# Four weight sums made by VectorE between the closing's steps instead of by GpSimd, and seven block products in another order

## The chip, the cores and the metric

One Trainium2 chip; the kernel runs on one of its cores, in one launch. The metric is the device time of that launch in microseconds, the median of several runs; lower is better.

## What is computed

Two graph layers on x (3327 rows of 1024 features) with a dense adjacency matrix. The first quantises a normalised x and a weight to few levels, multiplies them, and multiplies the adjacency matrix by the result. The second is attention with 8 heads of 64 features under the mask adj > 0, and then an MLP of four dense layers; its result is added to x1, the first layer's output. What matters for the change is the end of the second:

```python
att = softmax(where(adj > 0, leaky_relu(e_src + e_dst), NEG))
h   = elu(einsum('hnm,hmd->hnd', att, Wh))
enc = transpose(h, (1, 0, 2)).reshape(n, 512)
out = relu(enc @ W1.T + b1)        # 512 -> 256
out = relu(out @ W2.T + b2)        # 256 -> 256
out = relu(out @ W3.T + b3)        # 256 -> 512
return x1 + (out @ W4.T + b4)      # 512 -> 1024
```

## The kernel before

The 3327 rows are padded to 26 tiles of 128. Up to about 126 us the kernel makes the quantised support, up to about 900 us it multiplies by the adjacency matrix (line 730) and makes the heads' features, and from about 910 us it attends (line 1134). The MLP fills the rest, from 1918 us on. The four engines with queues of their own matter here: TensorE (PE), VectorE (DVE), ScalarE (ACT) and GpSimd (POOL); most DMAs are issued on the queue of SyncE (SP).

*Who sets the order.* The program is traced in Python, and a planner then orders each engine's instructions by readiness under costs of its own. An instruction that is not tied may be put ahead of earlier traced ones. `pin` (`tc.keep_in_program_order`) ties an instruction behind the one traced just before it on its engine; `issue_after` and `queue_behind` tie single pairs. [...]

*Attention.* `attends` (line 787) lists 32 steps: two halves of the target rows, four pairs of heads, the two heads of a pair, two sub-blocks of 6 or 7 row tiles. Each step runs over 26 source tiles: VectorE makes a selection `sel` from `srow`, `ndst` and the mask (line 1109), TensorE multiplies it into 6 or 7 accumulators (line 1134). At the end ScalarE copies these to `xs` (line 1152).

*Closing.* `close(i)` (line 924) is a generator that finishes a step, one piece for each call of `close_more` (line 976): VectorE adds the halves of `xs` to `su` (936) and ScalarE scales its upper half by `ratio` (939); VectorE forms `dn` (941); adds `up` (943); takes a reciprocal (946), with which ScalarE scales and goes through the elu (949, 951, 952); VectorE ends the elu (956), ScalarE splits the words (`eh`, 962), and GpSimd's queue writes them to `enc_d` in DRAM (964). All the VectorE pieces are pinned. Closings run during the next step; that of the last step has none behind it, and the loop at line 1155 runs it through, five calls.

*First group ahead.* During the last step the MLP's weights and biases are loaded and layer 1 of the first group of four row tiles is multiplied (`first_layer`, line 1058).

*MLP.* It goes by groups of four row tiles (the last has two). `dense` (line 1166) makes layers 1 to 3 with features on partitions; ScalarE evicts each 128 features from PSUM with bias and relu (line 1186). For the first group layers 2 and 3 are called ahead of the loop (lines 1280 and 1281), with `by_input=True`, which pins their matmuls. `joined` (line 1191) loads a later group's features from `enc_d` with two transposing DMAs (line 1039) and joins the half words with four ScalarE copies (line 1197). `load_x1` (line 1043) loads the rows of x1 into `nodes`; there are two buffers.

*Layer 4.* It takes two row tiles at a time in `rows_out` (line 1235). The two tiles and the two halves of the 512 inputs and of the 1024 outputs make a 2 x 2 by 2 x 2 block product, which is done with seven products of 128x512 outputs in place of eight ("1" to "7"). For that, four sums over the weight W4 are needed once: `t1` to `t4`, 128x1024 each (lines 1208 to 1211; `t1` overwrites a part of the weight, `t2` to `t4` lie where the last mask was, shown as "mask" in the profile), made by GpSimd; and four sums over the activations for each group, `combined` (line 1216), in the space of `enct0` (shown as "rest"). Each product is two passes over k in one of four PSUM banks (`o_ps`); the results are folded into the x1 rows `x11` to `x22`, to which the bias `bb4` is added first (line 1239), and `leave` (line 1245) makes an output half row and issues its DMA, on SP and, for an odd end of rows, on ScalarE's queue. Products "1", "6" and "5" are first copied to SBUF by ScalarE (line 1258), which frees their banks. `gaps` puts the next group's layers between the products.

Of the kernel before, what the change touches and what calls it, by code (L numbers as in the profile page):

```python
# [8 lines left out]
F32 = mybir.dt.float32  # L9
# [6 lines left out]
ALU = mybir.AluOpType  # L16
# [4 lines left out]
P = 128  # L21
# [4 lines left out]
F = 1024  # L26
KF = F // P
FC = F // 512
# [33 lines left out]
def two_layer_kernel(  # L62
# [23 lines left out]
    nc = tc.nc  # L86
# [81 lines left out]
    with tc.tile_pool(name="at", bufs=2, reuse_waits="tile") as atp:  # L168
# [42 lines left out]
        with tc.tile_pool(name="s1", bufs=2, reuse_waits="tile") as s1, tc.tile_pool(  # L211
# [9 lines left out]
            def pin(ins):  # L221
                tc.keep_in_program_order(ins)
# [574 lines left out]
    with tc.tile_pool(name="srow0", bufs=1, reuse_waits="tile") as srow0, tc.tile_pool(  # L797
# [178 lines left out]
        def close_more():  # L976
            if closing and closing[0][1] <= done:
                gen = closing[0][0]
                need = next(gen, None)
                closing[0] = gen, need  # L980
                if need is None:
                    closing.pop(0)
# [18 lines left out]
        for i, (c, g, e, si) in enumerate(attends):  # L1001
# [150 lines left out]
                freed = nc.scalar.copy(xs[:, b], accs[b].rearrange("p (q c) -> p q c", q=2))  # L1152
            gen = close(i)
            closing.append((gen, next(gen)))
        while closing:
            close_more()


    with tc.tile_pool(name="s4", bufs=2, reuse_waits="tile") as s4, tc.tile_pool(
        name="s4_ps", bufs=4, space=PSUM, reuse_waits="tile"  # L1160
    ) as ps_p, tc.tile_pool(name="s4_o", bufs=4, space=PSUM, reuse_waits="tile") as o_ps:

        enc_x1.append(nodes("nodes1"))
        groups = [range(t0, min(t0 + 4, T)) for t0 in range(0, T, 4)]

        def dense(xt, wt, bt, cols, tag, by_input=False):


            k_n, m_n = wt.shape[1], wt.shape[2] // P
            yt = s4.tile([P, m_n, 512], F32, tag=tag, name=tag)  # L1170
            order = [(k, m) for m in range(m_n) for k in range(k_n)]
            pss = {}
            for k, m in sorted(order) if by_input else order:
                if k == 0:
                    pss[m] = ps_p.tile([P, 512], F32, tag="ps", name=f"{tag}_ps")
                ins = nc.tensor.matmul(  # L1176
                    pss[m][:, :cols],
                    wt[:, k, m * P : (m + 1) * P],
                    xt[:, k, :cols],
                    start=(k == 0),  # L1180
                    stop=(k == k_n - 1),
                )
                if by_input:
                    tc.keep_in_program_order(ins)
                if k == k_n - 1:
                    nc.scalar.activation(
                        yt[:, m, :cols], pss[m][:, :cols], AF.Relu, bias=bt[:, m : m + 1]
                    )
            return yt

        def joined(g):

            load_encoded(g % 2, groups[g])
            xt = s4.tile([P, EMB // P, 512], F32, name="enct")
            n = len(groups[g]) * P
            for k in range(EMB // P):
                nc.scalar.copy(halves_of_words(xt[:, k, :n]), by_feature(enc_x1[g % 2][0], n)[:, :, k])  # L1197
            return xt

        w4c = [[w4[:, 2 * k : 2 * k + 2, c * 512 : (c + 1) * 512] for c in range(FC)] for k in range(2)]  # L1200
        t2, t3, t4 = (
            masks[1].rearrange("p b j i -> p (b j i)").bitcast(F32)[:, n * F : (n + 1) * F].rearrange(
                "p (k c) -> p k c", k=2
            )
            for n in range(3)
        )
        t1 = w4c[0][1]
        nc.gpsimd.tensor_tensor(t3, w4c[1][1], w4c[0][1], ALU.subtract)
        nc.gpsimd.tensor_tensor(t1, w4c[0][1], w4c[0][0], ALU.subtract)
        nc.gpsimd.tensor_tensor(t2, w4c[1][1], t1, ALU.subtract)  # L1210
        nc.gpsimd.tensor_tensor(t4, w4c[1][0], t2, ALU.subtract)
        sums = enct0.rearrange("p k c -> p (k c)").rearrange(
            "p (s k t i) -> p s k t i", s=4, k=2, t=2
        )

        def combined(h3, n):

            at = h3[:, :, : 2 * n * P].rearrange("p k (t e i) -> p k t e i", e=2, i=P)
            (a11, a21), (a12, a22) = [[at[:, 2 * k : 2 * k + 2, :, e] for e in range(2)] for k in range(2)]
            s1, s2, s3, s4_ = (sums[:, q, :, :n] for q in range(4))  # L1220
            nc.vector.tensor_tensor(s1, a21, a22, ALU.add)
            nc.vector.tensor_tensor(s2, s1, a11, ALU.subtract)
            nc.vector.tensor_tensor(s3, a11, a21, ALU.subtract)
            nc.vector.tensor_tensor(s4_, a12, s2, ALU.subtract)
            return {
                "1": (a11, w4c[0][0]),
                "2": (a12, w4c[1][0]),
                "3": (s4_, w4c[1][1]),
                "4": (a22, t4),
                "5": (s1, t1),  # L1230
                "6": (s2, t2),
                "7": (s3, t3),
            }

        def rows_out(tiles, x1, of, q, gaps):

            x0 = x1[:, q : q + 2]
            for e in range(2):
                nc.vector.tensor_tensor(x0[:, e], x0[:, e], bb4, ALU.add)
            (x11, x12), (x21, x22) = [  # L1240
                [x0[:, e, c * 512 : (c + 1) * 512] for c in range(FC)] for e in range(2)
            ]
            yo = [s4.tile([P, F], F32, name="yo", bufs=3) for _ in tiles]

            def leave(e, c, one, other):
                t, cs = tiles[e], slice(c * 512, (c + 1) * 512)
                nc.vector.tensor_tensor(yo[e][:, cs], one, other, ALU.add)
                for queue, r in zip((nc.sync, nc.scalar), row_pieces(t)):
                    queue.dma_start(out[t * P + r.start : t * P + r.stop, cs], yo[e][r, cs])

            kept = {b: s4.tile([P, 512], F32, name="p" + b, bufs=1) for b in "165"}
            for n, b in enumerate("1426573"):
                st, mv = of[b]
                ps = o_ps.tile([P, 512], F32, tag="o", name="o")
                for k in range(2):
                    nc.tensor.matmul(ps, st[:, k, q // 2], mv[:, k], start=(k == 0), stop=(k == 1))  # L1256
                if b in kept:
                    nc.scalar.copy(kept[b], ps)
                if b == "4":
                    nc.vector.tensor_tensor(x21, x21, ps, ALU.add)  # L1260
                elif b == "2":
                    nc.vector.tensor_tensor(x11, x11, ps, ALU.add)
                    leave(0, 0, kept["1"], x11)
                elif b == "6":
                    nc.vector.tensor_tensor(kept["6"], kept["6"], kept["1"], ALU.add)
                    nc.vector.tensor_tensor(x12, x12, kept["6"], ALU.add)
                elif b == "5":
                    nc.vector.tensor_tensor(x12, x12, kept["5"], ALU.add)
                    nc.vector.tensor_tensor(x22, x22, kept["5"], ALU.add)
                elif b == "7":  # L1270
                    nc.vector.tensor_tensor(kept["6"], kept["6"], ps, ALU.add)
                    leave(1, 0, kept["6"], x21)
                    leave(1, 1, kept["6"], x22)
                elif b == "3":
                    leave(0, 1, ps, x12)
                if n in gaps:
                    gaps[n]()

        encs = {1: joined(1)}
        h = dense(h1_0, w2, bb2, len(groups[0]) * P, "h2", by_input=True)  # L1280
        h3 = dense(h, w3, bb3, len(groups[0]) * P, "h3", by_input=True)
        for g, tiles in enumerate(groups):
            following = []
            if g + 1 < len(groups):
                load_x1((g + 1) % 2, groups[g + 1])
                if g + 2 < len(groups):
                    encs[g + 2] = joined(g + 2)
                following = [(w1, bb1, "h1"), (w2, bb2, "h2"), (w3, bb3, "h3")]
                h = encs.pop(g + 1)
            of = combined(h3, len(tiles) // 2)  # L1290

            def next_layer():
                nonlocal h
                wt, bt, tag = following.pop(0)
                h = dense(h, wt, bt, len(groups[g + 1]) * P, tag)

            at = [(0, 6), (1, 2), (1, 5)] if g == 0 else [(0, 2), (0, 6), (1, 2)]
            for pair in range(len(tiles) // 2):
                gaps = {n: next_layer for p, n in at if following and p == pair}
                rows_out(tiles[2 * pair : 2 * pair + 2], enc_x1[g % 2][1], of, 2 * pair, gaps)  # L1300
            h3 = h
# [43 lines left out]
```

## Time and profile before

| | us |
|---|---|
| runs, median of 3 | 2197.64 (2196.57 to 2198.72) |
| profiled execution, its own time | 2197.31 |
| its span, first to last instruction | 2195.4 |
| TensorE busy | 2154.9 |
| VectorE busy | 1627.1 |
| ScalarE busy | 1135.0 |
| GpSimd busy | 189.1 |
| last step's last matmul ends, layer 2 of the first group begins on TensorE | 1917.84 |
| first block product begins | 1936.69 |

The table and all the lines below come from one profiled execution. A timeline line has the start in us, the busy time, the engine, the line of the kernel and the operation, the tile written and the tiles read with their shapes, the number of instructions merged, and in brackets the idle time before it with what ended that.

### The profile page before, as it was taken

What the parts mean: (1) busy time and instruction counts of PE and PEld (TensorE: products, weight loads), DVE (VectorE), ACT (ScalarE), POOL (GpSimd) and SP (SyncE); (2) the same over time, 40 slices, a digit from 0 to 9 for tenths busy, and PEclk for the clock granted to TensorE, in tenths of its full rate; (3) what the DMA queues carried; (4) which work ended last, traced back from release to release, by engine and by line L of the source; (5) the groups of instructions that cost most, each with busy time, mean ns of one, the idle gap of its engine ahead of it and who ended that gap; (6) DMA issues with size and microseconds to landing.
All of it is one profiled execution on the core that took longest, in us unless ns stands there. A gap on an engine that the chain in (4) does not pass through costs nothing.

```text
span 2195.4 us, 31473 instructions
## 1 busy us (share of the span) xinstructions
PE 2154.9 (98%) x12405; PEld 1738.8 (79%) x12405; DVE 1627.1 (74%) x2144; ACT 1135.0 (52%) x1754; POOL 189.1 (9%) x273
## 2 busy tenths in 40 slices
PE   5999999999999999999999999999999999989999
PEld 2477777777777777799999999999999999834444
DVE  8845555554555555789999999999999999965445
ACT  6734445454454444466656656565656555452321
POOL 2301010111111101100000000000000000110000
PEclk9999999999999999999999999999999999999999
DMA  6654566556655556944242341655242332463222
GB/s 220 163 184 149 171 188 185 158 170 172 186 186 162 165 174 186 297 159 150 88 142 88 109 125 30 224 178 157 88 143 87 119 116 55 126 162 125 93 99 72
DMA packets 246036, 321.16 MB, mean 146 GB/s; under 512 B 105268, under 2 KB 187396, under 8 KB 245888
## 3 DMA queue, kind: packets, MB, share of 16 engines
q1 hardware_dynamic: 225276, 245.91, 36.9%
q0 software_dynamic: 20544, 73.18, 10.6%
q8 instruction: 97, 1.59, 0.3%
q14 instruction: 51, 0.42, 0.1%
q10 hardware_dynamic: 68, 0.06, 0.0%
HBM read 208.72 MB, written 86.79 MB: 135 GB/s over the span
## 4 chain that ended last, share of the span: by engine, by line
PE 86%; DVE 6%; DMA 5%; ACT 2%; issue 1%; SPq 0%; POOL 0%; DVEq 0%; ACTq 0%; POOLq 0%
PE acc L1134 29%; PE mm L730 22%; PE mps L883 15%; PE o L1256 7%; PE whm L641 6%; PE h_ps L1176 4%; PE mm L337 3%; DMA at<-in_adj_t 2%; DMA yht<-yh 2%; DVE lo L189 1%; DMA w<-in_w 0%; ACT enct L1197 0%; DVE prod L655 0%; DVE stats L141 0%; DVE fw L697 0%
## 5 line engine op out<-in xcount | busy, mean ns | idle before, releaser
L1109 DVE SCALAR_TENSOR_TENSOR sel<-srow,ndst,mask 128x896 fp32r<-128x896 f32 (+1 forms) x832 | 864.2, 1080 | 40.6 <-PE acc L1134 34.8
L883 PE MATMUL mps<-dw,mf 128*128 128x260 f32 x2704 | 453.6, 283 | 0.0
L730 PE MATMUL mm<-s_int,hi 128*128 128x512 f32 x1352 | 426.3, 396 | 0.0
L730 PE MATMUL mm<-s_int,lo 128*128 128x512 f32 x1352 | 416.7, 389 | 0.0
L1134 PE MATMUL acc<-f_even,sel 128*128 128x260 f32 x2704 | 396.8, 284 | 0.8 <-DVE sel L1109 0.8
L1134 PE MATMUL acc<-f_odd,sel 128*128 128x260 f32 x2704 | 394.1, 286 | 0.4 <-DVE sel L1109 0.4
L876 ACT CAST mf<-mask 128x1664 fp32r<-128x1664 uint8 x208 | 331.4, 1593 | 112.6 <-PE mps L883 98.3
L883 PEld LDWEIGHTS mps<-dw,mf 128*128 128x128 f32 x2704 | 377.5, 188 | 0.2 <-ACT part L897 0.2
L1134 PEld LDWEIGHTS acc<-f_odd,sel 128*128 128x128 f32 x2704 | 352.6, 188 | 7.9 <-issue 2.9
L1134 PEld LDWEIGHTS acc<-f_even,sel 128*128 128x128 f32 x2704 | 354.8, 188 | 4.2 <-DVE sel L1109 1.3
L730 PEld LDWEIGHTS mm<-s_int,hi 128*128 128x128 f32 x1352 | 253.9, 188 | 62.6 <-issue 11.5
L730 PEld LDWEIGHTS mm<-s_int,lo 128*128 128x128 f32 x1352 | 253.6, 188 | 53.1 <-DVE lo L189 0.3
L189 DVE TENSOR_TENSOR lo<-at,hi 128x896 fp32r<-128x896 f32 x104 | 106.2, 1021 | 156.3 <-ACT hi L185 156.2
L641 PE MATMUL whm<-whead,ht 128*128 128x512 f32 x416 | 182.7, 592 | 0.0
L190 DVE TENSOR_SCALAR mk<-at 128x896 uint8<-128x896 f32 (+1 forms) x104 | 61.5, 593 | 143.3 <-DMA at<-in_adj_t 143.3
L185 ACT CAST hi<-at 128x896 fp32r<-128x896 f32 x104 | 92.2, 887 | 131.6 <-PE mm L730 96.3
L641 PEld LDWEIGHTS whm<-whead,ht 128*128 128x128 f32 x416 | 78.8, 190 | 89.1 <-issue 87.1
L897 ACT COPY part<-mps 128x260 f32<-128x260 f32 x103 | 39.0, 379 | 189.6 <-PE mps L883 189.6
L964 POOL DMA_DIRECT2D enc_d<-eh x64 | 57.6, 904 | 901.6 <-ACT eh L962 901.1
L612 ACT COPY ht<-yht 128x1024 uint16<-128x1024 uint16 x50 | 67.7, 1355 | 72.8 <-DMA yht<-yh 72.8
L337 PE MATMUL mm<-w_int,xqt 128*128 128x512 bf16 x416 | 94.4, 383 | 6.6 <-DVE w_int L468 4.5
L648 ACT ACTIVATE wht<-whm,lnr 128x512 f32<-128x512 f32 x26 | 18.0, 691 | 144.4 <-PE whm L641 138.0
(195 smaller groups left out, 1894.2 us busy)
## 6 DMA issues: line engine op xcount, KB each, us to landing
feat_d<-fw POOLq DMA_DIRECT2D x26, 1040.0 KB, 5.3
f_even<-feat_d SPq DMA_DIRECT2D x7, 3380.0 KB, 13.8
f_odd<-feat_d SPq DMA_DIRECT2D x7, 3380.0 KB, 12.7
at<-in_adj_t SPq DMA_DIRECT2D x52, 448.0 KB, 4.3
at<-in_adj_t SPq DMA_DIRECT2D x52, 384.0 KB, 4.0
dw<-dsum_d SPq DMA_DIRECT2D x16, 910.0 KB, 9.2
dsum_d<-dw POOLq DMA_DIRECT2D x26, 520.0 KB, 6.2
x_d<-xt POOLq DMA_DIRECT2D x26, 512.0 KB, 6.7
```

The lines of the kernel that those rows point to most:

```text
L185: ins = nc.scalar.copy(hi, at)
L189: nc.vector.tensor_tensor(lo, at, hi.bitcast(F32), ALU.subtract)
L337: nc.tensor.matmul(mms[t][:, r], xqts[t][:, k, :], w_int[:, k, r], start=(k == 0), stop=(k == KF - 1))
L612: nc.scalar.copy(halves_of_words(ht[:, c * KF // FC : (c + 1) * KF // FC].rearrange("p k i -> p (k i)")), yht.rearrange("p (two k) i -> p ...
L641: ins = nc.tensor.matmul(whm, ht[:, k, :], whead[:, k, :], start=(k == 0), stop=(k == KF - 1))
L730: nc.tensor.matmul(mm[:, c * 512 : (c + 1) * 512], which[:, q, :], s_int[j][:, c * 512 : (c + 1) * 512], start=(j == 0 and which is hi), s ...
L876: ins = nc.scalar.copy(mf, mask[:, j : j + TH, :])
L883: nc.tensor.matmul(ps, mf[:, j % TH, :], dw[:, j, :], start=(j == 0), stop=(j == T - 1))
L1109: ins = nc.vector.scalar_tensor_tensor(sel[:, :nb], srow[:, :nb], ndst[:, j, h : h + 1], mask[:, :, j, :], ALU.is_gt, ALU.mult,)
L1134: ins = nc.tensor.matmul(accs[b], sel[:, b, :], f[:, j, :], start=(j == 0), stop=(j == T - 1))
L1176: ins = nc.tensor.matmul(pss[m][:, :cols], wt[:, k, m * P : (m + 1) * P], xt[:, k, :cols], start=(k == 0), stop=(k == k_n - 1),)
L1256: nc.tensor.matmul(ps, st[:, k, q // 2], mv[:, k], start=(k == 0), stop=(k == 1))
```

## The change

The weight sums go from GpSimd to VectorE and into the loop that ends the last closing: two ahead of its first call (line 936), none ahead of the second (941), one ahead of the third (943), none ahead of the fourth (946), one ahead of the fifth (956). They are pinned. So are the four sums over activations of each group and the additions of the bias to the x1 rows, which the planner could move before. The products' order goes from 1 4 2 6 5 7 3 to 1 4 2 6 7 5 3, and product "5" is no longer copied by ScalarE: VectorE adds it from PSUM, both times.

```diff
+        w4c = [[w4[:, 2 * k : 2 * k + 2, c * 512 : (c + 1) * 512] for c in range(FC)] for k in range(2)]
+        t2, t3, t4 = (
...
+        t1 = w4c[0][1]
+
+        def weight_sums():
+            for d, one, other in (
+                (t3, w4c[1][1], w4c[0][1]),
+                (t1, w4c[0][1], w4c[0][0]),
+                (t2, w4c[1][1], t1),
+                (t4, w4c[1][0], t2),
+            ):
+                pin(nc.vector.tensor_tensor(d, one, other, ALU.subtract))
+                yield
+
+        while len(closing) > 1:
+            close_more()
+        of_weight = weight_sums()
+        for n in (2, 0, 1, 0, 1):
+            for _ in range(n):
+                next(of_weight)
+            close_more()
         while closing:
             close_more()
...
-        nc.gpsimd.tensor_tensor(t3, w4c[1][1], w4c[0][1], ALU.subtract)
-        nc.gpsimd.tensor_tensor(t1, w4c[0][1], w4c[0][0], ALU.subtract)
-        nc.gpsimd.tensor_tensor(t2, w4c[1][1], t1, ALU.subtract)
-        nc.gpsimd.tensor_tensor(t4, w4c[1][0], t2, ALU.subtract)
...
-            nc.vector.tensor_tensor(s1, a21, a22, ALU.add)
-            nc.vector.tensor_tensor(s2, s1, a11, ALU.subtract)
-            nc.vector.tensor_tensor(s3, a11, a21, ALU.subtract)
-            nc.vector.tensor_tensor(s4_, a12, s2, ALU.subtract)
+            pin(nc.vector.tensor_tensor(s1, a21, a22, ALU.add))
+            pin(nc.vector.tensor_tensor(s2, s1, a11, ALU.subtract))
+            pin(nc.vector.tensor_tensor(s3, a11, a21, ALU.subtract))
+            pin(nc.vector.tensor_tensor(s4_, a12, s2, ALU.subtract))
...
-                nc.vector.tensor_tensor(x0[:, e], x0[:, e], bb4, ALU.add)
+                pin(nc.vector.tensor_tensor(x0[:, e], x0[:, e], bb4, ALU.add))
...
-            kept = {b: s4.tile([P, 512], F32, name="p" + b, bufs=1) for b in "165"}
-            for n, b in enumerate("1426573"):
+            kept = {b: s4.tile([P, 512], F32, name="p" + b, bufs=1) for b in "16"}
+            for n, b in enumerate("1426753"):
...
-                elif b == "5":
-                    nc.vector.tensor_tensor(x12, x12, kept["5"], ALU.add)
-                    nc.vector.tensor_tensor(x22, x22, kept["5"], ALU.add)
                 elif b == "7":
                     nc.vector.tensor_tensor(kept["6"], kept["6"], ps, ALU.add)
+                    nc.vector.tensor_tensor(x22, x22, kept["6"], ALU.add)
                     leave(1, 0, kept["6"], x21)
-                    leave(1, 1, kept["6"], x22)
+                elif b == "5":
+                    nc.vector.tensor_tensor(x12, x12, ps, ALU.add)
+                    leave(1, 1, ps, x22)
```

More of the change, by code (lines that the diff above doesn't have):

```diff
@@ L1154, in two_layer_kernel @@
             closing.append((gen, next(gen)))
+        w4c = [[w4[:, 2 * k : 2 * k + 2, c * 512 : (c + 1) * 512] for c in range(FC)] for k in range(2)]
+        t2, t3, t4 = (
+            masks[1].rearrange("p b j i -> p (b j i)").bitcast(F32)[:, n * F : (n + 1) * F].rearrange(
+                "p (k c) -> p k c", k=2
+            )
+            for n in range(3)
+        )
+        t1 = w4c[0][1]
[15 more added lines that the diff above has]
+            close_more()
         while closing:
@@ L1198, in joined @@
             return xt
[L1200 to L1208, printed above, removed]
-        nc.gpsimd.tensor_tensor(t1, w4c[0][1], w4c[0][0], ALU.subtract)
-        nc.gpsimd.tensor_tensor(t2, w4c[1][1], t1, ALU.subtract)
-        nc.gpsimd.tensor_tensor(t4, w4c[1][0], t2, ALU.subtract)
         sums = enct0.rearrange("p k c -> p (k c)").rearrange(
```

## The prediction

> **What bounds the kernel now.** First the page's busy shares and the chain of work that ended last:
>
> ```profile
> PE 2154.9 (98%) x12405; PEld 1738.8 (79%) x12405; DVE 1627.1 (74%) x2144; ACT 1135.0 (52%) x1754; POOL 189.1 (9%) x273
> ...
> PE 86%; DVE 6%; DMA 5%; ACT 2%; issue 1%; SPq 0%; POOL 0%; DVEq 0%; ACTq 0%; POOLq 0%
> ```
>
> TensorE sets the end. Nothing in the change takes a matmul away, so it can only win or lose time in which TensorE stands still or runs slowly. The stretches after the last attention step show where that is (PE, weight loads, DVE, ACT, POOL busy us, then granted clock, DMA share, GB/s):
>
> ```profile
> 1918.00:1937.00 19.00, 12.77 (x25) 5.09 (x26) 14.35 (x8) 7.97 (x23) 12.48 (x5) 0.91 0.00 0
> 1937.00:1958.00 21.00, 20.68 (x45) 8.70 (x44) 9.91 (x12) 12.30 (x14) 1.02 (x2) 0.92 0.83 206
> 1958.00:2178.00 220.00, 220.00 (x533) 101.22 (x534) 116.71 (x170) 66.79 (x98) 0.00 (x0) 1.00 0.35 109
> ```
>
> From 1958 to 2178 TensorE has no idle time at full clock: nothing to win there. From 1918 to 1958 it idles 6.55 us. The timeline of that stretch tells why:
>
> ```profile
> 1916.57 2.35 DVE L1239 TENSOR_TENSOR nodes<-nodes,rest 128x1024 f32<-128x1024 f32 x2
> 1916.74 4.39 POOL L1208 TENSOR_TENSOR mask<-weights 128x1024 f32<-128x1024 f32 x1 [0.60 <-DVE sel L1109]
> ...
> 1918.94 3.02 DVE L936 TENSOR_TENSOR su<-xs 128x780 f32<-128x780 f32 x1
> ...
> 1921.88 3.36 DVE L1239 TENSOR_TENSOR nodes<-nodes,rest 128x1024 f32<-128x1024 f32 x1
> ...
> 1923.44 1.24 ACT L1186 ACTIVATE h<-h_ps,rest 128x512 f32<-128x512 f32 x2
> 1924.16 8.65 PE L1176 MATMUL h_ps<-h,weights 128*128 128x512 f32 x16 [2.36 <-ACT h L1186]
> ...
> 1925.16 2.70 DVE L941 TENSOR_TENSOR su<-md,su 128x390 f32<-128x390 f32 x1
> ...
> 1927.78 3.36 DVE L1239 TENSOR_TENSOR nodes<-nodes,rest 128x1024 f32<-128x1024 f32 x1
> 1931.07 0.55 DVE L943 TENSOR_TENSOR su<-su 128x390 f32<-128x390 f32 x1
> ...
> 1934.62 0.56 DVE L956 SCALAR_TENSOR_TENSOR ht<-ex,ht 128x384 f32<-128x384 f32 x1 [2.78 <-ACT ex L952]
> 1935.21 0.83 ACT L962 COPY eh<-ht 128x768 uint16<-128x768 uint16 x1 [0.62 <-DVE ht L956]
> 1935.95 2.42 ACT L1186 ACTIVATE h<-h_ps,rest 128x512 f32<-128x512 f32 x4
> ...
> 1936.69 3.02 PE L1256 MATMUL o<-weights,h 128*128 128x512 f32 x4 [3.87 <-ACT h L1186]
> ```
>
> Read it as one chain. While GpSimd makes the four weight sums (1916.74 to 1930.06), VectorE's two-input instructions take 2.70 to 3.36 us; the same forms elsewhere take 1.23 (L1239), 0.97 (L936 in the head that was closed at 1859) and 0.56 (L941 at 1890.59). The bias additions of line 1239 were moved up between the closing's steps. So the last closing ends at 1936.04 (eh), and ScalarE, whose queue holds the evictions of layer 3 (L1186 x4) behind it, lets the first block product start at 1936.69, though layer 3 had ended on TensorE at 1932.8. The closing has a second customer: the feature transposes of the next groups, which wait for its write to enc_d. ScalarE's and TensorE's timelines show the end of that:
>
> ```profile
> 1947.65 9.71 ACT L1197 COPY enct<-nodes 128x1024 uint16<-128x1024 uint16 x8 [7.33 <-DMA nodes<-enc_d]
> 1957.22 1.07 ACT L1258 COPY p<-o 128x512 f32<-128x512 f32 x2
> ```
> ```profile
> 1957.85 1.98 PE L1256 MATMUL o<-weights,h 128*128 128x512 f32 x4 [0.32 <-ACT p L1258]
> ```
>
> Eight copies start when the transposes land, 11.6 us after eh's end, and the copies of products "6" and "5" stand behind them; TensorE waits 0.32 us for a bank. Last, the clock after the first gap, and the tail:
>
> ```profile
> 1924.50:1926.00 1.50, 1.50 (x2) 0.49 (x2) 1.50 (x2) 0.18 (x1) 1.50 (x1) 0.50 0.00 0
> ```
> ```profile
> 2189.12 1.29 DVE L1247 TENSOR_TENSOR yo<-p,nodes 128x512 f32<-128x512 f32 x2
> ...
> 2190.33 0.68 DVE L1247 TENSOR_TENSOR yo<-o,nodes 128x512 f32<-128x512 f32 x1
> ```
>
> [...] Here the clock is 0.50 after the gaps of 2.36 and 3.87 us and stays 1.00 after 0.32 and 0.77 us. [...]
>
> **The change, part by part.**
>
> *Sums off GpSimd.* Four sums of 128x1024 cost VectorE 4 x 1.15 us (two L1239 take 2.35). Two stand ahead of L936: 1916.65 to 1918.95, and L936 needs ScalarE's copies of the accumulators, which end at 1918.90: covered, and they replace two bias additions of the same length. One stands ahead of L943, beside ScalarE's scaling (L939, 1.54 us); one ahead of L956, beside ScalarE's 2.66 us of L949 to L952. Without such cover each costs its 1.2 us.
>
> *The closing.* L936 0.97, to 1919.92; L939 on ScalarE to 1921.5; then the layer-2 evictions, 1.24. Whether L941 must wait for L939 the trace doesn't show (a planned addition stood between), so I take both ends. Not: L941 to 1920.5, sum 2 to 1921.7, L943 to 1922.25, L946; ScalarE, free at 1922.8, needs 2.66; L956 at 1925.5, and with the 1.42 from there to eh's end, 1926.9. If it waits: L941 to 1922.1, sum to 1923.3, L946 at 1923.9, L949 at 1924.2, L956 at 1926.9, eh ends 1928.3. Before: 1936.04; 7.7 to 9.1 us earlier.
>
> *TensorE.* Layer 3 can start when the first layer-2 eviction ends, 1922.2 for 1924.16: the gap falls from 2.36 to 0.4 us, too short for the clock drop. At 7.03 us (as at 1971.69, pitch 6.87) it ends at 1929.1, and its evictions (from 1926.9 or 1928.3, four in 2.42) are in time for product "1", which needs two. First product 1929.1 for 1936.69: 7.6 us. The products at half clock (3.02 and 2.59 for 1.88) give 1.85 more.
>
> *The second customer.* Seven products (12.0) end at 1941.1, layer 1 of group 1 (6.87) at 1948.0. The transposes land at 1938.5 or 1939.9, the eight copies end at 1948.2 or 1949.6, the copy of "6" at 1948.8 or 1950.2, and the next product "1" needs its bank: 9.0 or 7.6 us before the 1957.85 of now. In the late case layer 1 also waits about 1 us for its fourth copy, inside that. "5" is no longer copied, so its bank comes free only after VectorE's chain: after "6" is copied, product "4" waits about 0.2 (VectorE adds 0.69, 0.6, 0.6), product "2" about 0.65 (four more additions of 0.6). Left: 8.1 or 6.8, mid 7.5.
>
> *Pinned sums and bias additions.* At a group's start VectorE now does four sums (2.5) and two additions (2.3) after the previous product "3", so product "4" is folded in 6.3 us after the group's first product starts; its bank is wanted at 8.6 (product "5") in the groups without a layer between (first and last), later elsewhere: 2.3 us of cover; in the first group, where the sums follow the last eviction (1929.5 or 1930.8), 1.6 or more. Cost nothing. "6" wants its sum at 5.15, ready at 2 to 3. For the x1 loads, which queue on SP behind output writes, the order of need is unchanged. GpSimd's removed instructions stood ahead only of the enc_d writes, and ended 6.3 us before those.
>
> *Order "6 7 5 3".* Thirteen ScalarE copies of 0.58 go; they were hidden. VectorE's eleven half-row additions per pair stay eleven. At the end, before, two additions (1.29) stand ahead of the last one, at 2190.33; now "5" has its output written before "3" comes, so the last addition waits only for TensorE (product end 2189.76 plus the 0.2 that L1262 waits after its own): 0.4 us. The last writes also start apart on the queues; I count nothing for that.
>
> Sum: 7.5 + 0.4 = 7.9 us off the profiled execution's 2197.31 (span 2195.4 and 1.9 around it): 2189.4. The median, 2197.64, lies 0.33 above, within the runs' spread; I forecast 2189.5. About 0.2% (4.4 us) is what a measurement can tell from no change.
>
> **The rivals.**
>
> *All recovered (inside the forecast).* If ScalarE's queue sets the copy of "6" ahead of the joined copies, idle 6.55, half clock 1.62 + 1.85 and tail 0.4 come back, less a 0.4 gap: 10.0, 2187.3.
>
> *Partial.* The planner sets the layer-2 evictions behind the closing on ScalarE. For: it is free to, and the closing's steps are now ready early. Against: it had them after L939 before. Then layer 3 starts at about 1927.5 after a long gap, at half clock first (8.65), and products at 1936.2; only half clock after the second gap, part of the bank waits and the tail return, 1.85 + 0.5 + 0.3 + 0.4: about 3 us, 2194.5, within 0.2%.
>
> *Slower.* The planner sets product 1's copy behind the joined copies. It decides when that copy isn't issued before the wait for the transposes. Then product "7", which needs that bank at 1936, stands until 1938.5 or 1939.9 + 9.7 + 0.6, mid 1949.5; the same product ran at 1945.35 before: 4.15 later, half clock again 1.7 (1.62 and 1.85 now), less today's 0.4 and the tail's 0.5: 5 us slower, 2202.5. [...] Against: before, the first copy went at 1939.74, ahead of the wait.
>
> **How the numbers follow.** Forecast with its faster end 0.78, partial 0.13, slower 0.09. Of the forecast nearly all lies between 2186.8 (10.0 us off and half a us of spread) and 2191.5; reaching to 2193.0 takes in a part of the partial case. Faster 0.79, same 0.12, slower 0.09.
>
> **What would show it.** No GpSimd work after 1918; L936 at 0.97 and L941 at 0.56 us; four 1.2 us sums from 1916.6 on; eh ending at 1927 to 1928; layer 3 starting near 1922.2 at clock 1.00; the first product near 1929; a wait of at most 1 to 2 us near 1948; from there to the end no idle. I am wrong if ScalarE's order changes, if VectorE's sums take over 2 us, or if a bank wait recurs in each pair of tiles.

## The result, and the profile after

| | before | changed | difference |
|---|---|---|---|
| median of 6 runs each, us | 2196.94 (2195.87 to 2198.72) | 2187.6 (2186.38 to 2190.65) | ratio 0.9958, 95% interval 0.9945 to 0.9971 |
| profiled execution, its own time | 2197.31 | 2187.28 | -10.0 |
| its span | 2195.4 | 2185.5 | -9.9 |
| first matmul of layer 2 begins | 1917.84 | 1917.55 | -0.3 |
| from there to the end of the span | 277.56 | 267.95 | -9.6 |

The last row is the measure that the rest of this text uses, and it is called **the stretch**: from the first layer-2 matmul of the first group to the end of the span. All that the change touches lies in it, but for the first weight sum, which begins 1.15 us ahead of it. The part ahead of it is not touched, yet it varied from 1916.5 to 1921.7 us over the profiles of this study, by more than several of the effects that are to be told apart.

The page of the changed kernel, busy shares and the chain that ended last:

```profile
PE 2151.5 (98%) x12405; PEld 1737.6 (80%) x12405; DVE 1622.2 (74%) x2148; ACT 1128.0 (52%) x1741; POOL 176.6 (8%) x269
...
PE 91%; DVE 4%; DMA 2%; ACT 2%; issue 1%; SPq 0%; POOL 0%; DVEq 0%; ACTq 0%; POOLq 0%
```

VectorE makes four instructions more and is not busier (1622.2 us for 1627.1): the four sums cost it 4.9 us, while L936, L941 and two bias additions, which had taken 12.4 us beside GpSimd's work, take about 4 us now. TensorE's share of the chain rose from 86 to 91%. The stretches by time, columns as in the prediction's table of stretches:

```profile
1918.00:1929.00 11.00, 10.54 (x25) 4.26 (x24) 5.79 (x8) 8.69 (x23) 1.65 (x2) 1.00 0.05 9
1929.00:1950.00 21.00, 21.00 (x50) 9.17 (x49) 9.10 (x13) 12.68 (x13) 0.00 (x0) 1.00 0.95 216
```

The granted clock is 1.00 throughout, and where TensorE had stood idle for 6.55 us between 1918 and 1958 it now does so for 0.46 up to 1950, and for 0.42 at the bank wait below. What GpSimd still does there (1.65 us) is the closing's two writes to enc_d. The timeline of the closing and of the first products:

```profile
1916.40 1.22 DVE L1172 TENSOR_TENSOR mask<-weights 128x1024 f32<-128x1024 f32 x1
...
1918.80 0.96 DVE L936 TENSOR_TENSOR su<-xs 128x780 f32<-128x780 f32 x1
1919.80 0.57 DVE L941 TENSOR_TENSOR su<-md,su 128x390 f32<-128x390 f32 x1
1919.80 1.55 ACT L939 ACTIVATE su<-su,ratio 128x65 f32<-128x65 f32 x6 [1.18 <-DVE su L936]
...
1921.97 7.13 PE L1202 MATMUL h_ps<-h,weights 128*128 128x512 f32 x16 [0.46 <-ACT h L1212]
...
1925.66 0.83 ACT L962 COPY eh<-ht 128x768 uint16<-128x768 uint16 x1 [0.63 <-DVE ht L956]
1928.94 1.88 PE L1270 MATMUL o<-weights,h 128*128 128x512 f32 x4
...
1937.26 9.68 ACT L1223 COPY enct<-nodes 128x1024 uint16<-128x1024 uint16 x8 [5.82 <-DMA nodes<-enc_d]
...
1947.83 1.88 PE L1270 MATMUL o<-weights,h 128*128 128x512 f32 x4
...
1952.09 1.98 PE L1270 MATMUL o<-weights,h 128*128 128x512 f32 x4 [0.42 <-DVE yo L1261]
```

The first two sums (L1172) end at 1918.88, when ScalarE's accumulator copies (L1152) have hardly ended (1918.62), so they cost L936 nothing to speak of. L936 took 3.02 us before and takes 0.96. L941 begins at the same moment as ScalarE's L939: it does not wait for it, which the prediction had left open. eh ends at 1926.49 instead of 1936.04, layer 3 begins after a gap of 0.46 us and runs at full clock, and no bracket stands behind the first product (1928.94): TensorE itself sets its time. The last line, product "2" of the next pair, shows a new wait, for a bank that VectorE now holds; product "4" ahead of it is late by 0.13 us for the same reason.

The 9.6 us can be read off from four of TensorE's instants. Layer 2 to the first product: 18.85 before, 11.39 after, 7.5 won. From there to the next pair's product "1": 21.16 and 18.89, 2.3 won. From there to the last product: 230.18 and 231.01, 0.8 lost. From the last product to the end: 7.37 and 6.66, 0.7 won.

### The profile page after: what moved, and what is told of

It is laid out like the page before. It is cut to its first block, busy times and chain, and to the rows that moved or that the text cites. A ratio compares the mean times of both kernels' runs of the same rounds, so it can differ in the third digit from the quotient of the medians.

```text
span 2185.5 us, 31479 instructions
## 1 busy us (share of the span) xinstructions
PE 2151.5 (98%) x12405; PEld 1737.6 (80%) x12405; DVE 1622.2 (74%) x2148; ACT 1128.0 (52%) x1741; POOL 176.6 (8%) x269
## 4 chain that ended last, share of the span: by engine, by line
PE 91%; DVE 4%; DMA 2%; ACT 2%; issue 1%; SPq 0%; POOL 0%; DVEq 0%; ACTq 0%; POOLq 0%
PE acc L1134 29%; PE mm L730 27%; PE mps L883 15%; PE whm L641 8%; PE o L1270 6%; PE h_ps L1202 4%; PE mm L337 2%; DVE sel L1109 1%; DMA xqt<-xq 0%; DMA w<-in_w 0%; DVE stats L250 0%; ACT enct L1223 0%; DMA at<-in_adj_t 0%; ACT xb L309 0%; DMA yht<-yh 0%
## 5 line engine op out<-in xcount | busy, mean ns | idle before, releaser
L1212 ACT ACTIVATE h<-h_ps,rest 128x512 f32<-128x512 f32 (+1 forms) x54 | 35.3, 655 | 112.6 <-PE h_ps L1202 112.4
```

## The experiments

**Theory A.** GpSimd's two-input sums and VectorE's two-input instructions keep each other waiting (L936 took 3.02 us beside them, 0.97 elsewhere), and the planner's moved bias additions lengthened that; the closing was late, TensorE stood idle (6.55 us from 1918 to 1958) and fell to half clock (granted 0.50 after the gaps of 2.36 and 3.87 us). Taking either away shortens the same chain. **Rival B:** the gain is that of the tied (pinned) additions and sums alone, and where the weight sums are made does not matter. **Rival C:** it is the new order of the products. In the table, the stretch is from one profiled execution each; the medians of the kernel before, beside which each ran, were 2197.29 (first four), 2196.85 (next four) and 2197.43 (last three).

| kernel | median us | ratio, 95% interval | first product | stretch |
|---|---|---|---|---|
| sums_only | 2191.61 | 0.9974, 0.9964 to 0.9985 | 1934.28 | 271.6 |
| pins_only | 2191.81 | 0.9974, 0.9963 to 0.9986 | 1933.79 | 272.3 |
| order_only | 2197.20 | 1.0001, 0.9993 to 1.0009 | 1935.96 | 277.6 |
| gpsimd_back | 2191.31 | 0.9975, 0.9966 to 0.9983 | 1937.61 | 271.5 |
| idle_gpsimd | 2195.80 | 0.9996, 0.9988 to 1.0004 | 1936.86 | 276.5 |
| four_first | 2190.52 | 0.9973, 0.9961 to 0.9985 | 1932.49 | 271.2 |
| sums_last | 2187.01 | 0.9954, 0.9942 to 0.9967 | 1927.78 | 268.1 |
| copy_first | 2186.14 | 0.9950, 0.9938 to 0.9963 | 1927.90 | 267.9 |
| changed_again | 2187.13 | 0.9953, 0.9940 to 0.9967 | 1929.09 | 267.9 |
| old_order | 2188.59 | 0.9960, 0.9948 to 0.9973 | 1930.92 | 267.7 |
| copies_tied | 2187.11 | 0.9953, 0.9940 to 0.9965 | 1929.70 | 267.0 |

**sums_only: the weight sums alone.** The changed kernel's `weight_sums` and its loop go into the kernel before; the activation sums and bias additions stay free, and the order stays "1426573".

> The weight sums alone go to VectorE, between the closing's steps; the bias additions and activation sums stay unpinned, the products keep their old order. In this kernel's order of instructions the planner puts an addition ahead of sums 1 and 2, one ahead of L941 and one ahead of L946. Theory A [...]: L936 at 0.97 but some 2.4 us later than in the changed kernel, eh ends near 1931 (before 1936.0, changed 1926.5), layer 3 still after a gap of over 2 us at half clock, first product near 1933; 5 to 6 us faster than before. Rival B (the pins did it, the move of the sums little): at most 3 us faster. Rival C (the new order of products did it): no faster than before.

The stretch is 5.9 us shorter than before, the time 0.26%. GpSimd is silent, so the two-input instructions are short, but the planner still sets the bias additions among the closing's steps, two ahead of L936 (1917.91 and 1920.18), one behind it and one behind L943:

```profile
1922.44 0.97 DVE L936 TENSOR_TENSOR su<-xs 128x780 f32<-128x780 f32 x1
...
1925.61 8.83 PE L1202 MATMUL h_ps<-h,weights 128*128 128x512 f32 x16 [2.48 <-ACT h L1212]
```

L936 begins 3.3 us after layer 2 does (1.25 in the changed kernel), and layer 3 still waits 2.48 us and runs its first part at half clock (granted 0.50 from 1926.6 to 1928.6; 8.83 us for 7.13). So rival B falls as the whole cause: with nothing else tied, the move by itself gives more than half of the gain. eh ended at 1933.31, later than expected even when counted from layer 2 (14.1 us after its start, for 18.2 before and 8.9 in the changed kernel), since ScalarE's queue had an eviction of layer 3 ahead of it; TensorE has no later wait to the end.

**pins_only: the ties alone.** The kernel before with `pin(...)` around the four sums of `combined` and the two bias additions, as in the diff above.

> Only the pins: activation sums and bias additions keep their traced order, the weight sums stay on GpSimd, the products keep their old order. Theory A: nothing stands between the closing's steps, but L936 and L941 still take 2.5 to 3 us beside GpSimd, and L943 now too; layer 3 starts as before near 1924.1 at half clock; eh ends near 1932, first product near 1932.8 as soon as layer 3 ends; 5 to 6 us faster. Rival B: 8 us or more faster. Rival C: no faster.

The stretch is 5.3 us shorter, about as expected, but by another path. The timeline:

```profile
1919.20 2.96 POOL L1209 TENSOR_TENSOR weights<-weights 128x1024 f32<-128x1024 f32 x1
1919.99 2.60 DVE L941 TENSOR_TENSOR su<-md,su 128x390 f32<-128x390 f32 x1
...
1927.70 6.26 PE L1176 MATMUL h_ps<-h,weights 128*128 128x512 f32 x10 [2.69 <-ACT h L1186]
```

L936 (1918.95) begins when GpSimd's L1208 is about to end (1919.13) and takes 1.00 us. L941 and L943, of half its size, take 2.60 and 2.52: L1209 ends at 1922.16 and L941 at 1922.59, L1210 ends at 1924.78 and L943 at 1925.21, both 0.43 us later. And layer 3 starts early, but the planner has put the second layer-2 eviction behind the closing's scaling, so TensorE waits 2.69 us in the middle of layer 3. I had expected one late start; half of the prediction's rival "partial" came instead.

**order_only: the order alone.** The kernel before with the changed kernel's loop over the products, "1426753" and "5" folded from PSUM.

> Only the products' order 1 4 2 6 7 5 3 and product 5 added from PSUM without ScalarE's copy. Theories A and B: the closing is as before; only the tail gains, 0.3 to 0.7 us faster. Rival C: most of the 9 us.

Nothing: ratio 1.0001, the stretch 277.59 for 277.56. The small gain that I expected is there and is spent again. From the last product to the end it is 6.68 us instead of 7.37, but in the first group TensorE now waits for banks that VectorE holds:

```profile
1958.86 1.98 PE L1256 MATMUL o<-mask,h 128*128 128x512 f32 x4 [0.26 <-DVE p L1268]
...
1961.26 1.98 PE L1256 MATMUL o<-weights,h 128*128 128x512 f32 x4 [0.42 <-DVE yo L1247]
```

One thing more is to be seen in this run. Its layer 3 ran at full clock (7.13 us, where it took 8.65 before), and still the first product comes 18.85 us after layer 2, as before. So half clock in layer 3 cost the kernel before nothing on the way to its first product; the closing's end set that.

**gpsimd_back: all but the move.** The changed kernel with the weight sums back on GpSimd at their old place, so ties and order stay.

> The changed kernel with the weight sums back on GpSimd at their old place (pins and new order kept). Theory A: as with the pins alone plus the tail, about 6 us faster than before, so 3 to 3.5 us slower than the changed kernel; L936, L941 and L943 at 2.5 to 3 us. Rival B: within 1 us of the changed kernel.

The stretch is 271.5 us, 3.6 longer than the changed kernel's. Its timeline is that of pins_only: L941 2.59 and L943 2.52 us beside GpSimd, layer 3 stopped for 2.70 us midway. Together with sums_only this gives the shape of the gain: sums alone 5.9, ties alone 5.3, with the order 9.6 in all. The two don't add up to 11.2, since both shorten one chain and the second finds less to take.

**idle_gpsimd: the same beside useless work.** In the changed kernel, GpSimd makes four subtractions of the weight sums' form into space that nobody reads; nothing waits for them.

```diff
+        for _ in range(4):
+            nc.gpsimd.tensor_tensor(spare, w4c[1][1], w4c[1][0], ALU.subtract)
         of_weight = weight_sums()
```

> The changed kernel, and GpSimd besides makes four subtractions of weight halves (128x1024, as large as the weight sums) into a spare space that nobody reads, from the last selection on. VectorE's and ScalarE's order is that of the changed kernel; no instruction of the closing needs them. Theory A (each of GpSimd's two-input instructions and VectorE's two-input instructions waits for the other's end): after sums 1 and 2 the two engines take turns, 2.2 us of GpSimd ahead of each of L936, L941, sum 3 and L943; eh ends near 1935 in place of 1926.5, and the time is 7 to 9 us above the changed kernel, near before. Rival (GpSimd delays only those who need its results): within 0.5 us of the changed kernel.

```profile
1917.92 12.31 POOL L1181 TENSOR_TENSOR mask<-weights 128x1024 f32<-128x1024 f32 x4 [0.60 <-DVE sel L1109]
...
1922.30 3.10 DVE L936 TENSOR_TENSOR su<-xs 128x780 f32<-128x780 f32 x1
1925.44 2.59 DVE L941 TENSOR_TENSOR su<-md,su 128x390 f32<-128x390 f32 x1
1927.61 9.35 PE L1207 MATMUL h_ps<-h,weights 128*128 128x512 f32 x16 [4.63 <-ACT h L1217]
```

This shows the effect by itself: GpSimd's work lengthens VectorE's though no result of it is awaited. 8.5 us are lost (276.48 less 267.95): L936 takes 3.10 us for 0.96, L941 2.59 for 0.57, the sums t1 and t2 3.25 and 3.36 for 1.22, the gap ahead of layer 3 is 4.63 us, and eh ends at 1936.22. That GpSimd's results came late for someone is no part of it. The 8.5 us are not GpSimd's share of the 9.6, for here VectorE's queue holds the weight sums besides, and two of these are lengthened too; that share is what sums_only and gpsimd_back bracket, 3.6 to 5.9 us. The 0.43 us from GpSimd's end to VectorE's end in pins_only, both times, fit two engines that take turns; what makes them do so is not in the traces.

**four_first and sums_last: do the places matter?** In the changed kernel, the weight sums all ahead of the closing's first step, or all behind its last.

```diff
-        for n in (2, 0, 1, 0, 1):
+        for n in (4, 0, 0, 0, 0):
```

> The changed kernel with all four weight sums ahead of the closing's first call, in place of two, none, one, none, one. Theory A (two sums have the cover of ScalarE's accumulator copies, more haven't): L936 starts 2.4 us later, near 1921.2; the layer-2 evictions, behind L939, and layer 3 follow, the gap reaches 2.9 us and the clock halves, 1.7 us more; first product near 1933; 4 us slower than the changed kernel. Rival (any place on VectorE is as good, since the gain is GpSimd's absence): within 0.5 us of it.

```profile
1923.82 8.83 PE L1202 MATMUL h_ps<-h,weights 128*128 128x512 f32 x16 [2.98 <-ACT h L1212]
```

Counted from layer 2, L936 is 2.5 us later, which is two sums without cover; the gap ahead of layer 3 grows from 0.46 to 2.98, half clock returns (granted 0.50 from 1925.8 to 1927.8; 8.83 us for 7.13), and the first product is 4.2 later. In the end 3.3 us are lost, not 4.2, because the bank waits of 0.8 vanish when TensorE comes later.

```diff
-        for n in (2, 0, 1, 0, 1):
+        for n in (0, 0, 0, 0, 0):
...
         while closing:
             close_more()
+        for _ in of_weight:
+            pass
```

> The changed kernel with the four weight sums after the closing, still ahead of the activation sums. Theory A: the closing's ends are set by ScalarE's chain, so eh ends as in the changed kernel; sum 4 ends near 1930.3 just ahead of product 4, which needs it at 1930.7; within 0.7 us of the changed kernel. Rival (the places between the steps earn something by themselves): 1 us or more slower.

The stretch is 268.07 us, 0.1 from the changed kernel's. The last sum, t4, is now made so late that TensorE stands idle 0.17 us for it ahead of product "4", which starts 0.33 us late; half of that comes back because layer 3 starts after a gap of 0.31 us and not 0.46:

```profile
1929.83 1.96 PE L1272 MATMUL o<-mask,h 128*128 128x512 f32 x4 [0.17 <-DVE mask L1172]
```

So in these profiles the careful places between the steps win nothing over "behind it all". What they must not do is to stand uncovered ahead of a step, as two of the four did in four_first.

**copy_first: the copy of "6" ahead of the joined copies.** In the changed kernel, `queue_behind(join, copied)` sets the eight joined copies of ScalarE behind the first pair's copy of product "6". It tests the prediction's steps on ScalarE's queue and on bank waits.

> The changed kernel with the first pair's copy of product 6 tied ahead of the joined copies on ScalarE. In the changed kernel that copy waits from 1936 to 1946.8 behind them, and the next pair's products 4 and 2 then wait 0.13 and 0.69 us for banks. Theory A: these waits go, no new ones come; 0.5 to 0.9 us faster than the changed kernel. Rival (the banks are wanted later anyway, or layer 1 then waits for its joined copies): no faster.

The two bank waits are gone, but the joined copies of a later group come ahead of the next layer-2 evictions instead, and TensorE waits there:

```profile
1961.24 7.13 PE L1202 MATMUL h_ps<-h,weights 128*128 128x512 f32 x16 [0.56 <-ACT h L1212]
```

The stretch is 267.89, 0.06 less. One wait was paid with another.

**changed_again, old_order, copies_tied.** The first is the changed kernel once more, beside the two others. old_order is the changed kernel with the order of before and "5" kept in SBUF; copies_tied is copy_first with one tie more:

```diff
+                with tc.issue_after(evicted["h2"].ins) if g == 3 else nullcontext():
+                    join = nc.scalar.copy(
```

> The changed kernel once more, beside the next two on the same chip: about 9 us faster than before.

> The changed kernel with the old products' order and product 5 copied by ScalarE again. By the run with the order alone, the new order earns 0.7 us at the tail and costs about as much in bank waits of the first group. Theory A: within 0.5 us of the changed kernel, its tail 0.7 us longer, its first group's waits of 0.82 us at most 0.3. Rival (without GpSimd's stall the tail counts in full): 0.7 us slower.

> As the run copy_first, and group 3's joined copies tied behind the layer-2 evictions of group 1, which in that run they held up (a wait of 0.56 us). Theory A: TensorE runs from layer 3 of the first group to the end without a wait; 0.7 to 0.9 us faster than the changed kernel, 0.5 than copy_first. Rival: another wait comes up, no faster than copy_first.

changed_again repeats the result: ratio 0.9953, the stretch 267.90 for 267.95. old_order has no bank wait in its first group and a tail of 7.31 us for 6.67, and its stretch, 267.67, is 0.2 shorter than the changed kernel's. Its median is 1.5 us above, but in the profiles that lies ahead of the stretch (layer 2 starts at 1919.53 for 1917.70), where TensorE's queue is the same in both. In these profiles the order earns nothing, which order_only says too. What delayed the earlier part isn't known; going by the medians alone (ratios 0.9960 and 0.9953, each good to about 0.0013), the new order may be worth some 1.5 us or nothing. In copies_tied the list of TensorE's waits from 1919 to 2185 is down to this, in us in all, times and the longest:

```profile
PE h_ps L1204 <- ACT h L1214: 0.5, 1, 0.5
PE h_ps L1204 <- ACT xs L1152: 0.2, 1, 0.2
```

Its stretch, 266.99, is 0.9 shorter than changed_again's, as expected. Its median is not (2187.11 and 2187.13), for the earlier part took 0.6 longer in its profile. As a whole it isn't shown to be faster.

## Why the prediction was right, and where it was off

The forecast was 2189.5 with 2186.8 to 2193.0; the median is 2187.6. The cause is the predicted one; three terms of the sum were too small, all in the same direction.

- *Sums off GpSimd.* Predicted t3 and t1 from 1916.65 to 1918.95 under ScalarE's copies; measured 1916.40 to 1918.88, the copies to 1918.62. That they cost 1.2 us each without cover is shown by four_first: two uncovered sums made L936 2.5 us late.
- *The closing.* Two ends were given, 1926.9 and 1928.3 for eh. Measured 1926.49: the early one, since L941 did not wait for L939. Taking the middle cost the forecast about 0.65 us; the profile of before could not tell, since an addition stood between L936 and L941.
- *TensorE.* Layer 3 predicted at 1922.2 with a gap of 0.4, measured 1921.97 and 0.46; first product predicted at 1929.1, measured 1928.94; no half clock (granted 1.00 from 1921.97 to 1929), as predicted. Measured from layer 2, 7.5 us for the predicted 7.6.
- *The second customer.* Predicted 11.6 us from eh's end to the joined copies, as before; it was 10.8, so that they started at 1937.26 and the copy of "6" at 1946.81, early enough for the next pair's "1". That ran without a wait at 1947.83; predicted was 1948.8 even in the early case. Counted from layer 2, 9.7 us were won by then and not 9.0: 0.7 was missed. Of the chain, the two transposes took 6.8 us for 7.6, and the write and its issue 4.0 as before. Why the transposes were shorter was not tried; the prediction had no reason to expect it, so this part of the gain is luck.
- *Bank waits of "4" and "2".* Predicted 0.2 and 0.65; the products' starts lie 1.85 and 2.41 us after the ones before them, for a usual 1.72: 0.13 and 0.69. Right, and copy_first shows that their cause is the late copy of "6".
- *Pinned sums and additions.* Predicted to cost nothing. In the list of TensorE's waits after 1918 there are only the 0.46 and the 0.42 shown above.
- *The tail.* Predicted 0.4, measured 0.7 (7.37 to 6.66), but not by the predicted step. The last addition was to wait for TensorE alone. It does not: it is the second of the two in the last line here, begins at 2180.88, right behind the output of "5", and by the prediction's own sum TensorE would have let it start 0.1 us sooner:

```profile
2179.68 0.68 DVE L1286 TENSOR_TENSOR nodes<-nodes,o 128x512 f32<-128x512 f32 x1
2180.28 1.28 DVE L1261 TENSOR_TENSOR yo<-o,nodes 128x512 f32<-128x512 f32 x2
```

  From the last product's start to this addition it is 2.04 us, for 2.30 before: 0.26 won of the predicted 0.4. The rest, 0.44, lies behind the addition, from its start to the end (4.60 us for 5.04). That the last writes go out apart, which was counted at nothing, is the likely cause; it was not tried alone.

Sum: 7.9 predicted, 9.6 measured in the stretch: 0.65 for L941, 0.7 for the transposes and 0.3 for the tail (0.44 for its writes, less 0.14 at the addition) make the difference. Another 0.3 of the profiled executions' 10.0 is the earlier start of layer 2, which is chance.

*The rivals.* "All recovered" has the nearest time, 2187.3, and not its mechanism: the copy of "6" still stands behind the joined copies. Product "1" lost nothing by it because these came sooner; products "4" and "2" lost 0.8. "Slower" decides on product "1"'s copy; it was issued at 1930.86, 6.4 us ahead of the joined copies. "Partial" did not come in the changed kernel, but pins_only and gpsimd_back show that the planner does make such an order when the closing's steps are slow, so it was right to give it a chance.

What the prediction didn't see is how its parts share the gain. It named both the longer VectorE instructions beside GpSimd's sums and the bias additions between the closing's steps, left both out of the new chain, and gave one price for the two, 7.7 to 9.1 us; the ties appear in it only as something that costs nothing. The runs split the gain between GpSimd's silence and the ties, which keep the additions out from between the steps; either alone gives somewhat more than half. The new order, which was to bring 0.4 at the tail and to cost 0.85 in bank waits, brings nothing net.

## What to carry to other kernels

GpSimd looked free and was not free help here: beside its sums VectorE's two-input instructions on the path took 2.59 to 3.10 us for 0.57 to 0.96 (L941 and L936 in idle_gpsimd). Compare the duration of the same form with and without the neighbour at work, and follow what waits for it. Work taken over by the busy engine cost nothing here where another engine's time covered it, so look for the cover, and tie loose work that a planner could set between the steps of a chain. Gains that shorten one chain don't add up; try each alone as well as together, and where the untouched part of a program varies more than the effect, measure the stretch that the change touches.

## What the runs showed of the hardware that was not expected

**Strict turns.** In the kernel before, each of the four VectorE instructions with two inputs that began during one of GpSimd's sums ended a time after that sum which went by its own size. GpSimd's last three sums there:

```profile
1921.21 2.95 POOL L1209 TENSOR_TENSOR weights<-weights 128x1024 f32<-128x1024 f32 x1
...
1924.23 3.20 POOL L1210 TENSOR_TENSOR mask<-weights 128x1024 f32<-128x1024 f32 x1
...
1927.52 2.54 POOL L1211 TENSOR_TENSOR mask<-weights,mask 128x1024 f32<-128x1024 f32 x1
```

Set beside VectorE's lines in the prediction, VectorE ends 0.83, 1.08, 0.43 and 1.08 us after GpSimd's instruction (780, 1024, 390 and 1024 elements), each 0.13 or 0.14 less than the same form takes alone (0.97, 1.22, 0.57 and 1.22). So what they lost went by when GpSimd's sum ended: L936 took 3.02 us here and 1.00 in pins_only, where it began 0.18 us ahead of the end of L1208. GpSimd waits likewise: each of its four sums ends 2.19 to 2.21 us after the VectorE instruction ahead of it. So the first took 4.39 us, behind two bias additions, and 2.36 in gpsimd_back with none ahead. The reciprocal of line 946, which has one input, took 0.19 us beside L1211 in pins_only and 0.19 in the changed kernel, so this one was not held.

**The clock after a gap.** Gaps of 2.36 to 2.98 us ahead of or in layer 3 brought half clock in before, sums_only, pins_only, gpsimd_back and four_first (granted 0.50 in all but gpsimd_back, where the clock was not read and the ten matmuls after the gap took 6.25 us, for 6.26 in pins_only). One of 0.77 us did not (before, at 1893.89, where the clock stayed 1.00), nor did those of 0.42 and 0.46 us in the changed kernel. But in order_only the same gap of 2.36 did not, and a gap of 5.40 later did:

```profile
1923.43 7.13 PE L1176 MATMUL h_ps<-h,weights 128*128 128x512 f32 x16 [2.36 <-ACT h L1186]
```

The granted clock was 1.00 in the first 2 us after the one and 0.50 in those after the other, where the first product took 3.58 us for 1.88. Microsecond by microsecond, layer 3 of four_first shows more; its gap ended at 1923.82:

```profile
1923.80:1924.80 1.00, 0.98 (x3) 0.50 (x4) 0.19 (x1) 1.00 (x4) 0.00 (x0) 1.00 0.00 0
1924.80:1925.80 1.00, 1.00 (x3) 0.51 (x2) 0.00 (x0) 0.97 (x5) 0.00 (x0) 0.69 0.00 0
...
1927.80:1928.80 1.00, 1.00 (x3) 0.50 (x2) 0.00 (x0) 0.54 (x1) 0.17 (x1) 0.60 0.00 0
1928.80:1929.80 1.00, 1.00 (x3) 0.40 (x3) 0.00 (x0) 0.00 (x0) 1.00 (x2) 1.00 0.00 0
```

The two stretches left out show 0.50. A mean of 0.69 is 0.62 us at half clock, one of 0.60 is 0.80 us, so half clock lasted 0.62 + 2 + 0.80 = 3.4 us and began 1.4 us after TensorE had set to work again. In before the first half clock began at 1923.84, 0.32 us ahead of the end of its gap (1924.16):

```profile
1920.43:1923.84 3.41, 1.37 (x4) 0.30 (x2) 3.41 (x2) 1.85 (x7) 3.33 (x2) 1.00 0.00 0
1923.84:1927.25 3.41, 3.09 (x4) 1.51 (x5) 3.41 (x2) 0.84 (x2) 3.33 (x2) 0.50 0.00 0
```

The second began at 1937.49, 0.80 us after the end of its gap (1936.69), and the clock was 0.50 from there to 1940.90, again 3.41 us. So half clock did not come a fixed time after the end of a gap, and a gap of 2.36 us brought it in before and not in order_only. In these traces a gap's length alone does not decide; what else does is not shown, for no run moved a gap of one length in time.
